# Filling the waits of the first spectral-norm chain and of the first batch's entry with other products, and splitting the first loads of a four-layer convolution and attention kernel

## The chip, the cores and the metric

The kernel runs on one NeuronCore of a Trainium2 chip. The metric is the device time of one execution in microseconds (us). The kernel before takes 1958.89 us (median of three runs, 1958.59 to 1959.13). The profile is one execution of 1957.9 us. Engines are called PE (TensorE, with its weight loads as PEld), DVE (VectorE), ACT (ScalarE), POOL (GpSimd) and SP (SyncE, which here only issues transfers).

## The reference, cut to what matters

Four layers run one after the other on `x` of shape (8, 512, 32, 32) in float32. Only the first two matter for the change:

```python
# layer 0
f = relu(batchnorm(conv1x1(x, Wf)))          # 64 channels, 1024 positions, statistics over the batch
g = relu(batchnorm(conv1x1(x, Wg)))
h = conv1x1(x, Wh)
z = einsum('bcn,bcm->bnm', f, g)             # per batch item
attn = z / svd(z).largest
x = conv1x1(einsum('bnm,bcm->bcn', attn, h), Wv) + x
# layer 1: group norm, then attention over 1024 positions with 512 channels
h = group_norm(x); q, k, v = wq h, wk h, wv h
x = x + wp (softmax(q^T k * scale) applied to v)
# layer 2: a second attention with 128 channels; layer 3: a convolution with signs of x and of its weights
```

## The kernel before, in words

**First pass.** The eight batch items are loaded one after the other (`load_x`, four transfers of 512 KB each, one for each 128 channels, on the SP queue) and multiplied by the three small weights: `fg` for f and g and `h` for h (the loop over `b` with `products`, L1131). For item 0 the loop runs over the four channel chunks outside and over f, g, h inside, so that PE can begin with the first chunk. The weights `fg` (256 KB) and `h` (128 KB) come over the ACT queue, in that order. The results of f and g stay in SBUF, their batch statistics are collected on the way.

**Preparation of layer 1.** Layer 1 uses two folded matrices: `wu`, the product of `wq` and `wk`, and `wo`, the product of `wv` and `wp`. For this `wq`, `wk` and `wv` are first turned (`natural`, eight 128x128 transposes into a two-bank PSUM tile `wide`, then one copy to SBUF), and then multiplied (`product`, L1187: 16 products of 128x128 by 128x512 each; a copy of 128x1024 after each eight, the first on ACT, the second on DVE). `biases` makes two bias vectors with 16 products each that have a single column (L1207, L1222). The main part multiplies in seven block products instead of eight, so it needs sums and differences of the blocks of `wu` and `wo`: `sums_of`, four DVE instructions (L298 to L301).

**The chain.** The largest singular value comes from powers of a 128x128 matrix that holds two batch items: `chain` squares it 2 x 11 times. One step is two products (L935, L936), two copies out of PSUM, one on DVE and one on ACT (L949, L951, or with a scale L953, L957), and then the next step. Every second step is scaled: there a trace goes through a product with a mask (L969), a copy (L970), a reciprocal and two squares on DVE (L996, L997, L999) before the copies may run. There are four such chains; the first one must be finished before the first batch item can enter layer 1. The others run later, spread over the main part. The matrices themselves come from `turned_pair` (transposes of f and g, L1044, copies L1048 on ACT and L1050 on DVE) and `gram` (8 products of 128x128 each, L1241, and a DVE multiplication, L1250).

**The order of PE's work.** From the first chain to the end of the first entry PE's order is written by hand: the code inside `tc.manual_schedule` takes one step of the chain, then two pieces from a generator, `filler`, then the next step. A piece is, for the most part, two products of 128x512 halves or four to eight smaller ones. The other engines' orders are chosen by the framework's scheduler. The pieces come in the order in which `filler` yields them: transposes of `wv`, the product `wu`, the third matrix of the first pair (`gram`), the four sums of `wu` together with `scale_z`, both biases, the matrices of the three other pairs, the product `wo`, the four sums of `wo`.

**The entry.** `entering(0)` then brings the first batch item into layer 1: `weights0` (L274), four times two products and a DVE addition with statistics (`enter`, L393, L402, L405), two small products for the group means (L413, L420), and the square root. Between these steps PE takes the rest of the pieces. After it come the normalization of the item (`normal`, L441 on ACT, L443 on DVE), the differences of its blocks (`split_h`, L309 to L312) and `make_u`, 28 products (L370), with which the main part begins. PSUM holds two `wide` tiles and four single banks in this part.

Of the kernel before, what the change touches and what calls it, by code (L numbers as in the profile page):

```python
# [12 lines left out]
ALU = mybir.AluOpType  # L13
# [70 lines left out]
def kernel(  # L84
# [30 lines left out]
    def wide():  # L115
        return psum["wide"].tile([P, N], F32, tag="wide", name="wide")
# [15 lines left out]
    def load_x(b):  # L132
        t = xpool.tile([P, CC, N], F32, tag="x", name="xt")
        src = x[b].rearrange("(cc p) n -> p cc n", p=P)
        for cc in range(CC):
            nc.sync.dma_start(out=t[:, cc, :], in_=src[:, cc, :])
        return t

    def half(i):
# [16 lines left out]
    early = ctx.enter_context(ExitStack())  # L156
    psum_pools(early, 2, 4)
    a1 = early.enter_context(tc.tile_pool(name="a1", bufs=1))
    load_w("fg", w_fg, [P, CC, P], a1, nc.scalar)
    first = load_x(0)  # L160
    load_w("h", w_h, [P, CC, MID], a1, nc.scalar)


# [934 lines left out]
    def scale_z():  # L1098
# [6 lines left out]
        nc.vector.tensor_tensor(sbw["z"], sbw["z"], ps, ALU.mult)  # L1105


    later = {
        1: [("w3", w_3, a1)],
        2: [("q", w_q, a1)],  # L1110
# [10 lines left out]
    for b in range(B):  # L1121
        xt = load_x(b) if b else first
        for name, src, pool in later.get(b, ()):
            load_w(name, src, shapes.get(name, [P, CC, C]), pool)
        if b >= B - 2:
            resident[b] = xt
        banks = [bank() for _ in w0]

        def products(i, cc):
            for h in range(NH):  # L1130
                mm(  # L1131
                    out=banks[i][side(h), :],
                    lhsT=w0[i][:, cc, :],
                    rhs=xt[:, cc, half(h)],
                    start=cc == 0,
                    stop=cc == CC - 1,
                )

        if b == 0:
            for cc in range(CC):  # L1140
                for i in range(3):
                    products(i, cc)
        for i in range(3):
            if b:
                for cc in range(CC):
                    products(i, cc)
            if i == 0:
                nc.scalar.copy(fs[b], banks[i])
                nc.vector.bn_stats(st[:, 0, b, :], fs[b])
# [12 lines left out]


    nat = {}

    def natural(name, tag):
        t = nat[name] = a1.tile([P, CC, C], F32, tag=tag, name="nat_" + name)
        for i in range(CC // 2):
            tp = wide().rearrange("p (o c j) -> p o c j", o=2, j=P)
            for k in range(2):  # L1170
                for cc in range(CC):
                    nc.tensor.transpose(
                        tp[:, k, cc, :], sbw[name][:, cc, bass.ts(2 * i + k, P)], ident
                    )
            dst = t[:, 2 * i : 2 * i + 2, :].rearrange("p o (c j) -> p o c j", j=P)
            if i % 2:
                nc.vector.tensor_copy(dst, tp)
            else:
                nc.scalar.copy(dst, tp)
            yield  # L1180

    def product(lt, rhs, dst):
        for i in range(CC // 2):
            ps = wide()
            for k in range(2):
                for oc in range(CC):
                    mm(  # L1187
                        out=ps[:, half(k)],
                        lhsT=lt[:, oc, bass.ts(2 * i + k, P)],
                        rhs=rhs[:, oc, :],  # L1190
                        start=oc == 0,
                        stop=oc == CC - 1,
                    )
                    if k == 0 or oc < CC - 1:
                        yield
            to = dst[:, 2 * i : 2 * i + 2, :].rearrange("p o c -> p (o c)")
            if i % 2:
                nc.vector.tensor_copy(to, ps)
            else:
                nc.scalar.copy(to, ps)  # L1200
            yield

    def biases():
        ps = bank()
        for cc in range(CC):
            for oc in range(CC):
                mm(  # L1207
                    out=ps[:, cc : cc + 1],
                    lhsT=nat["k"][:, oc, bass.ts(cc, P)],
                    rhs=col("L1_conv_bq", oc),  # L1210
                    start=oc == 0,
                    stop=oc == CC - 1,
                )
            if cc == 1:
                yield
        nc.vector.tensor_copy(bu, ps[:, 0:CC])
        yield

        ps = bank()
        for oc in range(CC):  # L1220
            for cc in range(CC):
                mm(  # L1222
                    out=ps[:, oc : oc + 1],
                    lhsT=sbw["p"][:, cc, bass.ts(oc, P)],
                    rhs=bvc[:, cc : cc + 1],
                    start=cc == 0,
                    stop=cc == CC - 1,
                )
            if oc == 1:
                yield  # L1230
        nc.vector.tensor_tensor(bo, ps[:, 0:CC], vec("L1_conv_bp"), ALU.add)
        nc.vector.tensor_tensor(bvo, bo, vec("L0_conv_bv"), ALU.add)
        yield

    def gram(j, i, lt, rhs):
        ps = bank()
# [39 lines left out]
    nat_q = natural("q", "w3")  # L1279
    next(nat_q)  # L1280
# [20 lines left out]
    for i in range(2):  # L1301
        for k in range(2):
            relu(2 * jl + k, i)
    next(nat_q)
    nat_k = natural("k", "q")
    next(nat_k)
    next(nat_k)

    def filler():

        yield from natural("v", "k")
        load_w("p", w_p, [P, CC, C], a1, tag="v")
        yield from product(nat["q"], nat["k"], wu)
        yield from gram(jl, 2, ht_pair[jl], gtl)
        cols2 = [slice(0, C // 2), slice(C // 2, C)]
        weights["u"] = sums_of(quarters_of(wu, chunks, cols2), [su[:, i] for i in range(3)])
        scale_z()
        yield
        yield from biases()
        for j in rest:  # L1320
            yield from grams(j)
        yield from product(nat["v"], sbw["p"], wo)
        weights["o"] = sums_of(quarters_of(wo, chunks, cols2), [so[:, i] for i in range(3)])

    todo = filler()
    for _ in range(5):
# [6 lines left out]

    relus = iter([(2 * j + k, i) for j in rest for i in range(2) for k in range(2)])
    with tc.manual_schedule(engines={mybir.EngineType.PE}):
        for _ in chain(jl, True):
            for _ in range(2):
                next(todo, None)
            for args in (next(relus, None),):
                if args:  # L1340
                    relu(*args)
        steps = entering(0)
        for k in range(CC + 2):
            next(steps)
            for _ in range(3 if k < CC else 5):
                next(todo, None)
        for _ in todo:
            pass
# [195 lines left out]
```

## Time and profile before

| | |
|---|---|
| time | 1958.89 us |
| PE busy | 1913.9 us of 1957.9 (98%) |
| DVE, ACT, POOL busy | 1151.2, 512.8, 223.9 us |
| mean granted PE clock | 0.991 |
| first pass, from the first product to the last of h | 5.3 to 96.2 us |
| first chain begins, its last trace product | 113.3 us, 182.2 us |
| first product of `make_u`, end of its last | 211.1 us, 237.3 us |

Busy time of PE includes time at a reduced clock, which the page shows apart ("PEclk"). A stretch in which PE is busy can therefore still be one in which it works at half speed. A matmul row of the profile is one of the passes of a float32 product; two rows make one product of the program.

### The profile page before, as it was taken

To read this page: it belongs to the slowest core of one execution; us is meant where nothing else is said; L and a number is where in the kernel's file an instruction comes from. 1 tells how busy PE (TensorE), PEld (TensorE's weight loads), DVE (VectorE), ACT (ScalarE), POOL (GpSimd) and SP (SyncE) were. 2 spreads that over 40 slices of the span, in tenths; PEclk is the share of its full clock that TensorE was granted. 3 is DMA by queue.
4 is the path that set the end of the run, shared out by engine and by line. 5 is a ranking of instruction groups with operands and counts; after the bars stand their busy time and mean duration, and the time that the engine had idled before them with its cause. 6 is when DMAs were issued, how large, how long until landed. Compare 5 with 4: busy or idle time off the path is not lost.

```text
span 1957.9 us, 16696 instructions
## 1 busy us (share of the span) xinstructions
PE 1913.9 (98%) x6230; PEld 989.2 (51%) x6230; DVE 1151.2 (59%) x1859; ACT 512.8 (26%) x811; POOL 223.9 (11%) x176
## 2 busy tenths in 40 slices
PE   8999899999999999999999999999999999999997
PEld 2377347454565446454455446444645445544653
DVE  3245667537774487637754577447663775466546
ACT  2132122125220342024211332025202421134114
POOL 1000001300021001210112001200120011201110
PEclk9989899999999999999999999999999999999999
DMA  9320000002000020001100120002000110010001
GB/s 337 130 76 1 6 6 12 1 11 86 6 12 1 11 86 17 1 1 46 56 11 0 33 70 12 1 11 86 11 0 1 51 46 11 0 33 22 11 1 56
DMA packets 26712, 66.99 MB, mean 34 GB/s; under 512 B 3760, under 2 KB 4016, under 8 KB 25984
## 3 DMA queue, kind: packets, MB, share of 16 engines
q1 hardware_dynamic: 25968, 65.09, 9.8%
q8 instruction: 51, 0.84, 0.2%
q0 software_dynamic: 224, 0.33, 0.1%
q10 hardware_dynamic: 432, 0.43, 0.1%
q14 instruction: 37, 0.30, 0.0%
HBM read 38.51 MB, written 18.87 MB: 29 GB/s over the span
## 4 chain that ended last, share of the span: by engine, by line
PE 93%; DVE 3%; ACT 2%; DMA 0%; issue 0%; POOL 0%; DVEq 0%; ACTq 0%
PE bank L370 43%; PE bank L537 20%; PE bank L883 6%; PE bank L761 6%; PE bank L1131 4%; PE bank L638 3%; PE bank L655 3%; PE bank L393 2%; PE bank L675 1%; PE bank L935 1%; PE wide L1187 1%; PE bank L1241 1%; PE bank L936 1%; PE bank L782 1%; PE quad L1044 1%; ACT both L699 0%
## 5 line engine op out<-in xcount | busy, mean ns | idle before, releaser
L537 PE MATMUL bank<-e,vt 128*128 128x512 f32 x768 | 334.0, 593 | 0.0
L537 PEld LDWEIGHTS bank<-e,vt 128*128 128x128 f32 x768 | 145.0, 190 | 175.4 <-issue 173.1
L370 PE MATMUL bank<-ut,h 128*128 128x512 f32 x384 | 183.4, 598 | 4.7 <-ACT e L332 4.7
L327 DVE TENSOR_TENSOR e<-bank,e 128x512 f32<-128x512 f32 x128 | 87.6, 684 | 61.5 <-PE bank L370 60.2
L370 PE MATMUL bank<-us,hs 128*128 128x512 f32 x256 | 121.3, 596 | 0.5 <-DVE us L299 0.5
L370 PEld LDWEIGHTS bank<-ut,h 128*128 128x128 f32 x384 | 70.6, 190 | 87.7 <-issue 73.5
L883 PE MATMUL bank<-e,tpg 128*128 128x512 f32 x256 | 114.6, 595 | 0.0
L761 PE MATMUL bank<-tpg 128*128 128x512 f32 x256 | 114.6, 592 | 0.0
L768 ACT ACTIVATE e<-bank 128x512 f32<-128x512 f32 x128 | 76.4, 597 | 128.5 <-PE bank L761 128.5
L370 PE MATMUL bank<-h,wu 128*128 128x512 f32 x192 | 92.1, 603 | 4.9 <-DVE h L443 4.9
L370 PE MATMUL bank<-wo,h 128*128 128x256 f32 x384 | 91.9, 382 | 0.0
L773 DVE TENSOR_TENSOR esum<-esum,e 128x1024 f32<-128x1024 f32 x48 | 58.8, 1225 | 54.9 <-ACT e L768 54.9
L342 POOL TENSOR_TENSOR e<-e 128x512 f32<-128x512 f32 x32 | 41.6, 1301 | 432.2 <-ACT e L321 361.3
L327 DVE TENSOR_TENSOR vt<-bank,vt 128x512 f32<-128x512 f32 x64 | 44.0, 687 | 69.6 <-PE bank L370 69.3
L883 PEld LDWEIGHTS bank<-e,tpg 128*128 128x128 f32 x256 | 48.0, 190 | 63.9 <-issue 63.9
L761 PEld LDWEIGHTS bank<-tpg 128*128 128x128 f32 x256 | 48.6, 190 | 60.7 <-issue 60.5
L370 PEld LDWEIGHTS bank<-wo,h 128*128 128x128 f32 x384 | 71.6, 190 | 14.3 <-ACT vt L321 4.9
L342 POOL TENSOR_TENSOR ut<-ut 128x512 f32<-128x512 f32 x16 | 21.8, 1362 | 477.7 <-ACT ut L323 477.7
L370 PEld LDWEIGHTS bank<-us,hs 128*128 128x128 f32 x256 | 47.3, 190 | 57.5 <-issue 51.4
L790 DVE RECIPROCAL rsum<-bank 128x512 f32<-128x512 f32 x16 | 53.7, 3355 | 30.3 <-PE bank L782 30.3
L665 ACT ACTIVATE sg<-xt,rb 128x512 f16<-128x512 f32 x64 | 43.7, 717 | 103.7 <-DVE xt L657 100.9
L1131 PE MATMUL bank<-xt,fg 128*64 128x512 f32 x256 | 58.6, 608 | 5.3 <-DMA fg<-in_w_fg 5.3
(321 smaller groups left out, 3084.4 us busy)
## 6 DMA issues: line engine op xcount, KB each, us to landing
xt<-in_x SPq DMA_DIRECT2D x56, 512.0 KB
out<-both SPq DMA_DIRECT2D x64, 256.0 KB
rfull<-rsum SPq DMA_DIRECT2D x64, 128.0 KB
f_dram<-f SPq DMA_DIRECT2D x8, 256.0 KB
fb<-f_dram SPq DMA_DIRECT2D x8, 256.0 KB
w<-in_w SPq DMA_DIRECT2D x1, 1024.0 KB
q<-in_w_q SPq DMA_DIRECT2D x1, 1024.0 KB
k<-in_w_k SPq DMA_DIRECT2D x1, 1024.0 KB
```

Source lines behind the costliest of these rows:

```text
L327: nc.vector.tensor_tensor(dst, ps, u, ALU.add)
L342: nc.gpsimd.tensor_tensor(c22, c22, c12, ALU.add)
L370: mm(out=ps[:, q * w : (q + 1) * w], lhsT=lt(ka, kb, q, k), rhs=rhs(ka, kb, q, k), start=first and q == 0 and k == 0, stop=last and k == 1 ...
L537: mm(out=ps, lhsT=a[:, t, bass.ts(r_, P)], rhs=e[t], start=first and t == 0, stop=last and t == NTH - 1, skip_group_check=True,)
L638: mm(out=ps[:, i, :], lhsT=xt[:, cc, bass.ts(4 * h + i, P)], rhs=sbw["tpg"][:, cc, 2 * P : 3 * P], start=cc == 0, stop=cc == CC - 1,)
L655: mm(out=ps, lhsT=sbw["z"][:, bass.ts(oc, P)], rhs=att, start=True, stop=True)
L761: mm(out=ps, lhsT=pt[:, 0, bass.ts(t, P)], rhs=tt[:, 0, half(h)], start=True, stop=True,)
L768: nc.scalar.activation(e[:, half(h)], ps, AF.Exp, scale=float(P) ** -0.5)
L773: nc.vector.tensor_tensor(esum, esum, e, ALU.add)
L790: nc.vector.reciprocal(r, ps)
L883: mm(out=banks[h], lhsT=gt[:, t, :], rhs=es[t][:, half(h)], start=t == 0, stop=t == NT - 1,)
L1131: mm(out=banks[i][side(h), :], lhsT=w0[i][:, cc, :], rhs=xt[:, cc, half(h)], start=cc == 0, stop=cc == CC - 1,)
```

## The change

Nothing of the computation is changed; the same products are made in another order.

- **First loads.** The first 512 KB of `x` come as two transfers of 256 KB (a half of the positions each), and `fg` as four transfers of 64 KB (one per channel chunk), so that the first product can begin when the first pieces have landed. `h` follows `fg` on the same queue as before.
- **`natural`** for `wq` runs inside the first pass, before the last item's products for h; the two halves of each turned tile are copied by ACT and DVE at the same time.
- **The chain's pieces.** After a step without a scale PE takes one piece, after a scaled step two. The sums of `wu` are issued one by one between the pieces of the other pairs' matrices, and so are the biases, now in eight pieces of four products with a PSUM bank and a copy each.
- **`gram`** uses a `wide` tile in place of a single bank.
- **The entry.** Two pieces are taken after each of its first four steps and six after each of the last two, so that the product `wo` comes at the end. Both copies of `wo` are on ACT, and the sums of `wo` are issued after `make_u`.

```diff
-    load_w("fg", w_fg, [P, CC, P], a1, nc.scalar)
-    first = load_x(0)
+    fg = sbw["fg"] = a1.tile([P, CC, P], F32, tag="fg", name="fg")
+    for cc in range(CC):
+        nc.scalar.dma_start(out=fg[:, cc, :], in_=w_fg[:, cc, :])
+    first = load_x(0, True)
     load_w("h", w_h, [P, CC, MID], a1, nc.scalar)
...
         for i in range(3):
+            if b == B - 1 and i == 2:
+                for _ in natural("q", "w3"):
+                    pass
             if b:
...
-            if i % 2:
+            if i % 2 and vector:
                 nc.vector.tensor_copy(to, ps)
...
     def gram(j, i, lt, rhs):
-        ps = bank()
+        ps = wide()
...
-        yield from product(nat["q"], nat["k"], wu)
+        yield from product(nat["q"], nat["k"], wu, True)
         yield from gram(jl, 2, ht_pair[jl], gtl)
-        cols2 = [slice(0, C // 2), slice(C // 2, C)]
-        weights["u"] = sums_of(quarters_of(wu, chunks, cols2), [su[:, i] for i in range(3)])
         scale_z()
         yield
-        yield from biases()
+        between = biases()
+        sums = sums_u()
         for j in rest:
-            yield from grams(j)
-        yield from product(nat["v"], sbw["p"], wo)
-        weights["o"] = sums_of(quarters_of(wo, chunks, cols2), [so[:, i] for i in range(3)])
+            for _ in grams(j):
+                next(sums, None)
+                yield
+                if next(between, "end") != "end":
+                    yield
+        yield from product(nat["v"], sbw["p"], wo, False)
...
-        for _ in chain(jl, True):
-            for _ in range(2):
+        steps = entering(0)
+        for k, _ in enumerate(chain(jl, True)):
+            for _ in range(2 - k % 2 if k <= 2 * NSTEP else 4):
                 next(todo, None)
...
-            for _ in range(3 if k < CC else 5):
+            for _ in range(2 if k < CC else 6):
                 next(todo, None)
...
         ua = got[0]
+        weights["o"] = sums_of(quarters_of(wo, chunks, cols2), [so[:, i] for i in range(3)])
```

More of the change, by code (lines that the diff above doesn't have):

```diff
@@ L130, in psum_pools, with load_x @@
                 )
-    def load_x(b):
+    def load_x(b, split=False):
         t = xpool.tile([P, CC, N], F32, tag="x", name="xt")
@@ L135, in load_x @@
         for cc in range(CC):
-            nc.sync.dma_start(out=t[:, cc, :], in_=src[:, cc, :])
+            for ns in [half(h) for h in range(NH)] if split and not cc else [slice(0, N)]:
+                nc.sync.dma_start(out=t[:, cc, ns], in_=src[:, cc, ns])
         return t
@@ L1105, in scale_z, with natural @@
         nc.vector.tensor_tensor(sbw["z"], sbw["z"], ps, ALU.mult)
+    nat = {}
+    def natural(name, tag):
+        t = nat[name] = a1.tile([P, CC, C], F32, tag=tag, name="nat_" + name)
+        for i in range(CC // 2):
+            tp = wide().rearrange("p (o c j) -> p o c j", o=2, j=P)
+            for k in range(2):
+                for cc in range(CC):
+                    nc.tensor.transpose(
+                        tp[:, k, cc, :], sbw[name][:, cc, bass.ts(2 * i + k, P)], ident
+                    )
+            dst = t[:, 2 * i : 2 * i + 2, :].rearrange("p o (c j) -> p o c j", j=P)
+            nc.scalar.copy(dst[:, 0], tp[:, 0])
+            nc.vector.tensor_copy(dst[:, 1], tp[:, 1])
+            yield
     later = {
@@ L1161, with product @@
             scale_signs(total3)
[L1164 to L1175, printed above, removed]
-            if i % 2:
[L1177 to L1182, printed above, removed]
+    def product(lt, rhs, dst, vector):
         for i in range(CC // 2):
@@ L1196, in product @@
             to = dst[:, 2 * i : 2 * i + 2, :].rearrange("p o c -> p (o c)")
-            if i % 2:
+            if i % 2 and vector:
                 nc.vector.tensor_copy(to, ps)
@@ L1203, in biases @@
     def biases():
-        ps = bank()
[L1205 to L1214, printed above, removed]
-                yield
[L1216 to L1231, printed above, removed]
+        for w, rhs, dst in (
+            (nat["k"], [col("L1_conv_bq", k) for k in range(CC)], bu),
+            (sbw["p"], [bvc[:, k : k + 1] for k in range(CC)], bo),
+        ):
+            for i in range(CC):
+                ps = bank()
+                for k in range(CC):
+                    mm(
+                        out=ps[:, 0:1],
+                        lhsT=w[:, k, bass.ts(i, P)],
+                        rhs=rhs[k],
+                        start=k == 0,
+                        stop=k == CC - 1,
+                    )
+                if dst is bu:
+                    nc.vector.tensor_copy(bu[:, i : i + 1], ps[:, 0:1])
+                else:
+                    nc.vector.tensor_tensor(
+                        bo[:, i : i + 1], ps[:, 0:1], col("L1_conv_bp", i), ALU.add
+                    )
+                yield
         nc.vector.tensor_tensor(bvo, bo, vec("L0_conv_bv"), ALU.add)
-        yield
     def gram(j, i, lt, rhs):
-        ps = bank()
+        ps = wide()
         for t in range(NT):
@@ L1278 @@
         nc.vector.bn_aggr(mv[:, i, :], st[:, i, :, :])
-    nat_q = natural("q", "w3")
-    next(nat_q)
+    nat_k = natural("k", "q")
+    next(nat_k)
     turn(last[0], last[1], ht_pair[last[0] // 2], 0)
@@ L1303, with sums_u @@
             relu(2 * jl + k, i)
-    next(nat_q)
-    nat_k = natural("k", "q")
     next(nat_k)
-    next(nat_k)
+    def sums_u():
+        a11, a12, a21, a22 = quarters_of(wu, chunks, cols2)
+        s1, s2, s4 = (su[:, i] for i in range(3))
+        weights["u"] = {
+            "A11": a11, "A12": a12, "A22": a22, "S1": s1, "S2": s2, "S3": a21, "S4": s4
+        }
+        for args in (
+            (s1, a21, a22, ALU.add),
+            (s2, s1, a11, ALU.subtract),
+            (a21, a11, a21, ALU.subtract),
+            (s4, a12, s2, ALU.subtract),
+        ):
+            nc.vector.tensor_tensor(*args)
+            yield
+    cols2 = [slice(0, C // 2), slice(C // 2, C)]
     def filler():
@@ L1312, in filler @@
         load_w("p", w_p, [P, CC, C], a1, tag="v")
-        yield from product(nat["q"], nat["k"], wu)
+        yield from product(nat["q"], nat["k"], wu, True)
         yield from gram(jl, 2, ht_pair[jl], gtl)
-        cols2 = [slice(0, C // 2), slice(C // 2, C)]
-        weights["u"] = sums_of(quarters_of(wu, chunks, cols2), [su[:, i] for i in range(3)])
         scale_z()
         yield
-        yield from biases()
+        between = biases()
+        sums = sums_u()
         for j in rest:
-            yield from grams(j)
-        yield from product(nat["v"], sbw["p"], wo)
-        weights["o"] = sums_of(quarters_of(wo, chunks, cols2), [so[:, i] for i in range(3)])
+            for _ in grams(j):
+                next(sums, None)
+                yield
+                if next(between, "end") != "end":
+                    yield
+        yield from product(nat["v"], sbw["p"], wo, False)
     todo = filler()
@@ L1341 @@
                     relu(*args)
-        steps = entering(0)
         for k in range(CC + 2):
             next(steps)
-            for _ in range(3 if k < CC else 5):
+            for _ in range(2 if k < CC else 6):
                 next(todo, None)
```

## The prediction

> **What bounds the kernel.** Page first: PE is busy 1913.9 of 1957.9 us and is 93% of the chain that ended last, so the time is PE's work plus PE's waits plus what the clock takes. The instruction order on the engines shows that from the first scores on, PE and DVE of the changed kernel follow the old order, so I look only at the first 240 us. The view of busy time by stretches (us; then busy time and instructions of PE, PEld, DVE, ACT, POOL; granted clock; DMA share; GB/s):
>
> ```profile
> 0.00:5.30 5.30, 0.03 (x2) 0.03 (x2) 0.06 (x1) 1.28 (x1) 4.32 (x14) 1.00 0.65 205
> 5.30:9.00 3.70, 3.65 (x8) 0.74 (x8) 0.00 (x0) 0.00 (x0) 0.45 (x13) 1.00 1.05 289
> 9.00:96.20 87.20, 87.17 (x413) 30.03 (x413) 27.79 (x68) 13.88 (x23) 2.03 (x2) 1.00 0.63 237
> 96.20:113.30 17.10, 14.96 (x113) 12.45 (x111) 8.02 (x23) 12.81 (x18) 0.70 (x1) 1.00 0.45 131
> ...
> 135.30:152.40 17.10, 16.30 (x77) 15.85 (x77) 3.75 (x16) 1.49 (x4) 0.00 (x0) 0.50 0.00 0
> 152.40:182.20 29.80, 29.10 (x245) 27.16 (x243) 16.24 (x64) 6.83 (x18) 0.00 (x0) 1.00 0.01 1
> 182.20:202.40 20.20, 19.01 (x50) 6.89 (x50) 13.98 (x28) 4.03 (x6) 0.00 (x0) 1.00 0.04 14
> 202.40:211.20 8.80, 0.85 (x6) 0.68 (x5) 7.64 (x28) 0.75 (x2) 1.20 (x1) 0.76 0.00 0
> 211.20:217.20 6.00, 5.58 (x7) 1.95 (x8) 5.55 (x7) 2.76 (x5) 0.00 (x0) 0.50 0.00 0
> 217.20:237.30 20.10, 20.10 (x48) 8.98 (x47) 4.64 (x8) 3.33 (x5) 2.52 (x2) 1.00 0.00 0
> ```
>
> Three losses: PE idle to 5.3 us; 17.1 us at half clock in the chain; 8 us without work at 202 to 211, with half clock after it. The list of PE's waits names the releasers:
>
> ```profile
> PE bank L1131 <- DMA fg<-in_w_fg: 5.3, 1, 5.3
> PE bank L370 <- DVE h L443: 4.9, 1, 4.9
> PE bank L420 <- DVE dev L417: 2.5, 1, 2.5
> PE bank L1207 <- DVE z L1105: 1.4, 1, 1.4
> ...
> PE bank L274 <- DVE gm L1014: 0.9, 1, 0.9
> ```
>
> For the first loads, the queue table of the transfer view for 5 to 6 us and for 8 to 9 us (packets, MB, share):
>
> ```profile
> q1 hardware_dynamic: 69, 0.28, 69.4%
> q10 hardware_dynamic: 73, 0.07, 21.0%
> ```
> ```profile
> q1 hardware_dynamic: 62, 0.23, 70.8%
> q0 software_dynamic: 62, 0.07, 25.8%
> q10 hardware_dynamic: 65, 0.02, 9.1%
> ```
>
> q1 carries SP's x in 4 KB packets, q10 what ACT issued in small ones. Both get as many packets in the same time, whatever their size.
>
> **The Trainium skill.** "TensorE: Matmul & The Clock Gate", Part 1, says PE runs at half clock until a window of about 3.4 us was busy, and falls back after an idle one. The trace agrees: full clock from 9.0 us, half clock at 135.3 to 152.4 and 207.0 to 217.2, which are five and three times 3.41 us. "DMA: Bandwidth & Descriptors", "Queues, rings and completion order", says each DMA engine goes round the queues packet by packet; the rows above agree. The TensorE page, in its architectural detail, says ACT and DVE take instructions strictly in order; no row here contradicts it, and I use it for what queues behind a wait.
>
> **Part 1, first loads.** For item 0 PE's order is four products with fg, two with h, then the next chunk. fg's pieces begin it earlier, but h decides when it goes on: before, PE's loads of h weights wait until 9.03 us. h is behind fg on ACT's queue. Per DMA engine fg was 8 packets of 2 KB; now it is 32 of 512 B, each taking turns with a packet of x. So h's 8 packets end beside x's last chunk (16 turns of 2 KB and 24 of 4 KB), not its second. By then x 2.10 MB, fg 0.26, h 0.13 and most of POOL's 0.33 MB have moved, 2.8 MB. The transfer rates of before for each us (0.17 MB by 3 us, then 0.41, 0.39, 0.41, 0.10, 0.36, 0.33, 0.26, 0.29 MB) make 2.7 MB by 11 us, so the estimate is 11.4. Before, the last packet of h ended at 8.1 and PE saw it at 9.03, so add 0.9: 12.3 us. The four products need 3.7 us at half clock as before, begin about 4.2 and end near 8; PE idles over 4 us and restarts at half clock for one window, which costs 3.4/2 = 1.7 us. Sum (12.3 - 9.0) + 1.7 = +5.0 us. Bounds: h at 9.0 as before, with nothing gained, 0; if h drained freely because x's queue ran dry, PE would begin 1 us sooner, -1; one more cold window, +6.5. After it PE never waited for x up to 96 us, and x has more time now.
>
> **Part 2, natural q.** Its 16 transposes (2.1 us) move ahead of h's 3.65 us, and each turned tile now leaves by a 0.56 us ACT copy beside a 0.69 us DVE copy in place of one of 1.01 or 1.23. The waits of the transposes (1.2 and 0.4 us) go, but the statistics (mean, power on POOL, relu on ACT) still end about 8.6 us after h's products against 8.0 us of PE work. Net -0.5 us.
>
> **Part 3, chain to end of make_u.** Before: 113.3 to 237.3 us = 124.0. PE's idle time in it is 12.5 us (in four stretches 0.59 + 0.83 + 0.8 + 0.7, then 1.19 + 7.95 + 0.42) and half clock costs 16.3/2 + 5.6/2 = 10.9 us. Work at full clock: 124.0 - 23.4 = 100.6 us. The products are the same, so this stays, and I count the new waits.
>
> *Pace of the chain.* An unscaled step needs 1.05 us from its first product to the next (118.15 to 119.2), a scaled one 2.05 (154.90 to 156.95). A piece is 0.86 to 0.93 us. PE has 0.44 + 0.9 = 1.3 us in the first and 0.44 + 0.2 + 1.8 = 2.4 in the second, so nothing waits unless DVE is late by more than 0.3 to 0.4 us. The chain and the pieces inside it are 44 us of PE work (23 pairs of 0.44, 12 trace products of 0.2, 34 pieces), not the 69 us from 113.3 to 182.2. The single-column biases, 7 us of work drawn out to 12.4 at half clock, now come 0.9 us at a time between denser products, so I expect full clock.
>
> *What queues on DVE in it.* Three instructions of 0.65 us (two sums of wu and z) stand between trace, reciprocal and squares of one scaled step: 1.3 us of wait. Two bias copies stand ahead of a reciprocal and wait for a piece's end: 0.65 each. A gt copy of 0.69 us ahead of a square: 0.85. The 1.2 us copy of wu, ft copies and the rest: five times 0.25. Together 4.7 us. ACT's relus (0.76 us each) at the start repeat what was there before.
>
> *End of the chain.* From the last trace product to L274 took 3.06 us; 3.6 us of matrices cover it. What remains is 0.5 us for the pv copies, and 0.3: 0.8.
>
> *Entry.* Each of four steps costs DVE 0.75 + 0.69 + 0.73 + 0.69 + 0.21 = 3.07 us; now ft, gt and mask copies, 2.5 us together (2 x 0.69, 4 x 0.29), lie between them. DVE needs about 15.8 us to the last statistics, PE has 4 x 1.06 (L393) + 5.4 (six half matrices) + 2.1 (transposes) = 11.7 of work and holds four banks only, so it waits 4.1.
>
> *Means and root.* The two waits of 2.5 and 4.9 us go: five pieces of wo (4.3 us) stand before L420's product and eleven (9.5 us) after it, against about 5 us for the rest.
>
> *Switch to make_u.* A new wait. Both wo copies are on ACT, the second can start only after the last wo product, and ACT's four h instructions (0.73 each) queue behind it. From that product's end: copy to 1.2 us, chunk 1 at 2.0, its other half at 3.4; DVE, which also has sums of wo in front of L309, makes L309 to 4.7, a sum to 5.4, L310 to 6.6. PE has four products, 3.4 us, so 3.2 are waits. They are short enough to keep the clock.
>
> Sum of new waits 4.7 + 0.8 + 4.1 + 3.2 = 12.8 us against 23.4 of idle and clock before: -10.6 us. Bounds: waits of 8 us (-15) or 17 us (-6).
>
> **Sum.** 1958.9 + 5.0 - 0.5 - 10.6 = 1952.8 us.
>
> **Rivals.**
> *The loads do no harm.* If h lands at 9 us or fg's pieces even gain 1 us, parts 2 and 3 stand alone: 1958.9 - 11.1 - 0.5 = 1947.3 us. For it: only 384 KB on ACT's queue, and DMA at 1 in the first 50 us is a mean. Against: the equal packet counts. Chance 0.30.
> *The clock falls in the chain or the entry, slower than before.* If one-column products count as idle, or the entry's waits fill a window, two spells at half clock as long as the old ones (17.1 and 10.2 us) return their 10.9 us, with loads 5 worse: 1952.8 + 10.9 = 1963.7 us. For it: the clock fell just as biases began. Against: 68% busy windows (182 to 202) kept it, and biases are now a quarter of the work. Chance 0.13.
> *One spell of half clock, or waits at the upper bound*: +4.5 us, 1957.3 us. Chance 0.12.
> The likeliest, 1952.8, has 0.45.
>
> **How the numbers follow.** Around the likeliest the part bounds give 1949 to 1957. A range of 1944.5 to 1959 leaves out the slow rival and little of the fast one's edge. 0.2% is 3.9 us, so faster means below 1955.0: three quarters of the likeliest (0.34), the fast rival (0.30), a sliver of the third: 0.66. Same: the rest of the likeliest (0.11), most of the third and some of the slow one: 0.22. Slower: 0.12.
>
> **What would show it.** The start: PE's wait for h near 12 us, and half clock after it (wrong if the steady run begins at or before 9). First pass 5 us later as a whole. In the chain: 23 steps in 47 to 51 us with clock 1.00, waits for ACT's cur at the steps named. No wait for L443's h, but one for L441's, and for L310's hs. If wo's copies or biases show a spell at 0.50, the second or third rival holds.

## The result, and the profile after

The changed kernel takes 1948.65 us (median of four runs, 1948.13 to 1950.19) against 1958.94 us of the kernel before (1958.59 to 1959.13): 10.3 us less, a ratio of 0.9949 with the 95% interval 0.9932 to 0.9966. The forecast was 1952.8 us in a range of 1944.5 to 1959.0, with faster as the likeliest outcome. Direction and range hold; the gain is larger than the 6.1 us forecast.

Where did it go? With the matmuls of both traces laid side by side from the last one backwards, every one from the first scores product on (238.70 us before, 226.84 us after) comes 11.7 to 11.9 us sooner. So the whole difference arises in the first 240 us. Behind the last matmul 0.7 us is lost again: the last DVE instruction ends 4.7 us before the end of the span before (1953.2 of 1957.9) and 5.4 us after (1941.4 of 1946.8). So the two profiled executions lie 11.1 us apart, and the medians 10.3: the execution of before that was profiled is one of its slower ones (an execution with a span of 1957.9 us on record took 1959.7 us).

The busy time by stretches of the changed kernel (us; then busy time and instructions of PE, PEld, DVE, ACT, POOL; granted clock; DMA share; GB/s), cut at the events that answer those of before:

```profile
4.50:10.10 5.60, 4.30 (x8) 1.43 (x8) 0.00 (x0) 1.28 (x1) 1.24 (x15) 1.00 0.95 244
10.10:99.06 88.96, 88.95 (x429) 31.92 (x430) 29.00 (x70) 15.05 (x25) 2.03 (x2) 1.00 0.61 234
99.06:115.00 15.94, 14.39 (x95) 10.67 (x95) 6.97 (x24) 11.46 (x18) 0.70 (x1) 1.00 0.50 169
115.00:162.70 47.70, 45.76 (x319) 37.77 (x319) 28.47 (x117) 14.92 (x35) 0.55 (x1) 1.00 0.06 22
162.70:168.20 5.50, 4.84 (x37) 3.89 (x37) 2.59 (x10) 2.70 (x5) 0.00 (x0) 1.00 0.01 3
168.20:182.50 14.30, 12.47 (x80) 8.81 (x80) 12.98 (x27) 1.17 (x2) 0.00 (x0) 1.00 0.06 19
182.50:199.50 17.00, 16.99 (x44) 8.35 (x44) 2.29 (x14) 1.01 (x1) 1.02 (x1) 0.90 0.00 0
199.50:204.00 4.50, 2.31 (x6) 0.68 (x5) 4.38 (x9) 4.30 (x6) 0.00 (x0) 1.00 0.00 0
204.00:226.80 22.80, 22.75 (x52) 9.73 (x53) 11.30 (x17) 3.33 (x5) 2.53 (x2) 1.00 0.00 0
```

Read it from the top. The clock records begin at 9.01 us, and the view prints 1.00 for the time ahead of them. PE was at half clock there: eight rows with `fg` took 3.68 us in the kernel before up to 9.0 us and 1.88 us afterwards. PE starts 0.8 us sooner than before, then idles 1.3 us ahead of 10.1 us, and the first pass ends at 99.06 us with the 1.75 us of turned `wq` inside it. The chain (115.0 to 162.7 us) is 47.7 us long at full clock, where the old one took 69 us with 17 us at half clock in it. The entry (168.2 to 182.5 us) waits 1.8 us, there is a short spell of reduced clock behind it (the 0.90), and the 8 us hole at 202 to 211 us of before has become 2.2 us (4.50 - 2.31). The list of PE's waits up to 245 us:

```profile
PE bank L1151 <- DMA fg<-in_w_fg: 4.5, 1, 4.5
PE bank L416 <- DVE mv L415: 1.8, 1, 1.8
PE bank L373 <- ACT ut L335: 1.5, 1, 1.5
PE bank L1151 <- DMA h<-in_w_h: 1.3, 1, 1.3
PE quad L1047 <- DVE z L1108: 0.7, 1, 0.7
PE bank L373 <- DVE h L446: 0.7, 1, 0.7
```

The wait of 2.5 us for the deviations is gone, and that for DVE's h has shrunk from 4.9 to 0.7 us. The wait at the group means (L416, L413 before) has grown from 0.6 to 1.8 us. New are 1.5 us in `make_u` for a copy that stands behind h on ACT, and 1.3 us for the weights h of the first pass. For the last one, the queue table of the transfer view for 7 to 8 us (packets, MB, share):

```profile
q10 hardware_dynamic: 236, 0.14, 50.6%
q1 hardware_dynamic: 41, 0.13, 39.2%
```

q10 is ACT's queue with the small pieces of `fg` and h, q1 is SP's with `x`. Here the small packets did not take turns one for one: nearly six of them went for each packet of `x`. Over 5 to 9 us it was 453 against 182, two and a half for each.

### The profile page after: what moved, and what is told of

The parts are those of the page before. It is cut to its first block, busy times and chain, and to the rows that moved or that the text cites. A ratio compares the mean times of both kernels' runs of the same rounds, so it can differ in the third digit from the quotient of the medians.

```text
span 1946.8 us, 16715 instructions
## 1 busy us (share of the span) xinstructions
PE 1908.0 (98%) x6230; PEld 982.9 (50%) x6230; DVE 1149.2 (59%) x1867; ACT 514.4 (26%) x815; POOL 223.6 (11%) x176
## 4 chain that ended last, share of the span: by engine, by line
PE 93%; DVE 3%; ACT 2%; issue 0%; DMA 0%; ACTq 0%; POOL 0%; DVEq 0%
PE bank L373 43%; PE bank L540 20%; PE bank L886 6%; PE bank L764 6%; PE bank L1151 4%; PE bank L641 3%; PE bank L658 3%; PE bank L396 2%; PE wide L1191 1%; PE bank L678 1%; PE bank L938 1%; PE bank L939 1%; PE bank L785 1%; PE wide L1238 1%; DVE st L408 0%; ACT up L701 0%
```

## The experiments

Medians are device times of several runs beside the kernel before on the same chip (1958.8 to 1959.3 us there). The changed kernel was measured once, beside 1958.94 us of the kernel before, so differences to it compare separate measurements, between which the kernel before itself differs by up to 0.5 us. In the texts quoted, "theory" is the view of the prediction or its correction, "rival" the other one.

### The first loads: four kernels

The first one is the kernel before with only the two splits of the first loads:

```diff
-    load_w("fg", w_fg, [P, CC, P], a1, nc.scalar)
-    first = load_x(0)
+    fg = sbw["fg"] = a1.tile([P, CC, P], F32, tag="fg", name="fg")
+    for cc in range(CC):
+        nc.scalar.dma_start(out=fg[:, cc, :], in_=w_fg[:, cc, :])
+    first = load_x(0, True)
```

> The kernel before with nothing but the split loads of item 0 and of fg. Theory (the weights h land later, since fg's small packets stand ahead of them): first product about 4.5 us, PE's wait for h ends near 10.1 us in place of 9.0, all later work 1.1 us later, 1960.0 us. Rival (an earlier first product is what counts): 0.8 us faster, 1958.1 us. Second rival (what was predicted: h at 12.3 us and a restart at half clock): 5 us slower, 1964 us.

Measured: 1960.02 us (twelve runs, 1957.94 to 1961.31), ratio 1.0002 (0.9994 to 1.0011). No difference can be told. In the trace h comes at 9.99 us, PE waits 1.8 us for it, and the first pass and the chain run 0.95 us late; at the switch the half clock lasts 6.8 us in place of 10.2, which in that execution pays it back.

The second is the changed kernel with the old loads, that is the same diff turned round:

> The changed kernel with the loads of before: fg in one transfer, x in four. Theory: h is awaited until 9.0 us, chain and entry keep what they gained, 1.1 us faster than the changed kernel, 1947.5 us. Rival (the loads are part of the gain): 0.8 us slower than the changed kernel, 1949.4 us.

Measured: 1945.54 us (1945.17 to 1946.33), ratio 0.9931 (0.9914 to 0.9947): 3.1 us faster than the full change. Laid side by side, the first pass comes 0.66 us sooner than in the changed kernel: PE goes on with h at 8.62 us without a wait, but is at half clock until 10.39 us. Another 1.67 us come in one step behind the entry, where the changed kernel's spell of half clock is missing (last section), and 0.65 us behind the last matmul.

The third keeps the splits but sends h right behind the first piece of `fg`:

```diff
     for cc in range(CC):
         nc.scalar.dma_start(out=fg[:, cc, :], in_=w_fg[:, cc, :])
+        if cc == 0:
+            load_w("h", w_h, [P, CC, MID], a1, nc.scalar)
     first = load_x(0, True)
-    load_w("h", w_h, [P, CC, MID], a1, nc.scalar)
```

> The changed kernel, with h loaded right behind the first piece of fg and ahead of the three others. Theory: h lands by 6 to 7 us, before the four products that run at half clock have ended near 8 us, so PE goes on without a wait from 4.5 us; full clock at 9.0 us as before; steady work begins about 0.7 us sooner than before the change and 1.8 us sooner than in the changed kernel, 1946.8 us. Rival (the DMA engines are simply full, so whatever comes first delays the rest): the wait moves to another piece, no gain against the changed kernel, 1948.6 us.

Measured: 1947.32 us (1945.98 to 1948.47). PE's wait for h is gone from its list of waits, and the profiled execution, which has the same spell of half clock as the changed kernel's, runs 1.1 us ahead of it throughout.

The fourth leaves `fg` whole and splits only `x`:

> The changed kernel with fg in one transfer and only x's first chunk in two. Theory: h stands behind 8 packets of fg per engine again, PE's wait for h ends at 8.5 to 9.0 us, 1.1 to 1.6 us faster than the changed kernel, 1947.2 us. Rival (it is x's smaller packets that bring h late, by making more turns): h near 10 us, no difference, 1948.6 us.

Measured: 1946.50 us (1945.48 to 1947.36), with 1947.36 in the profiled execution, again with the spell; it is 1.0 us ahead of the changed kernel throughout.

What follows: the harm of the split loads is h's lateness, about 1 us, and comes from the pieces of `fg` in front of it. It is much less than the 5.0 us forecast, because PE waited 1.3 us and not over 4, and in this execution the clock was not lost. Splitting `x` shows neither harm nor gain.

That the clock was kept is luck. In the six traces with `fg` split and h last, h comes between 9.49 and 10.30 us. The latest one (the kernel of "The second copy of `wo` on DVE" below) waits 2.2 us for it and loses the clock for one window:

```profile
7.47:10.89 3.42, 1.18 (x7) 0.30 (x6) 0.00 (x0) 0.00 (x0) 0.00 (x0) 1.00 1.08 287
10.89:14.30 3.41, 3.41 (x12) 0.98 (x10) 1.23 (x9) 0.00 (x0) 0.92 (x1) 0.50 1.02 380
```

Its first pass ends at 100.95 us, 1.9 us later than the changed kernel's.

### The place of `natural` for `wq`

The changed kernel with the transposes of `wq` and their undivided copies back between the statistics:

```diff
-            if b == B - 1 and i == 2:
-                for _ in natural("q", "w3"):
-                    pass
...
-    nat_k = natural("k", "q")
-    next(nat_k)
+    nat_q = natural("q", "w3")
+    next(nat_q)
```

> The changed kernel with the transposes of wq after the first pass, as before, and the old copies of 1.01 and 1.23 us. The trace of the changed kernel has 0.6 us more between the end of the first pass (less the 1.75 us of transposes) and the chain's start than the kernel before. Theory (the earlier transposes bring nothing, since the statistics set the chain's start, and the finer copies lie among them on DVE): 0.5 us faster than the changed kernel, 1948.1 us. Rival (the prediction's: the waits of the transposes go): 0.5 us slower, 1949.1 us.

Measured: 1948.66 us (1948.06 to 1950.51) against 1948.65: no difference. In its trace the transposes wait 1.2 and 0.4 us for DVE's copies, as before the change, but from 14 us to the middle of the chain the distance to the changed kernel only goes from 1.38 to 1.47 us. The waits came and went without a trace in the sum. The 1.38 us themselves come from the start, where this execution has full clock only from 12.93 us; behind the entry it has no spell of half clock and gets 1.5 us back.

### The pieces in each step of the chain

The changed kernel with two pieces after every step and three or five in the entry, the counts of before:

```diff
-            for _ in range(2 - k % 2 if k <= 2 * NSTEP else 4):
+            for _ in range(2):
...
-            for _ in range(2 if k < CC else 6):
+            for _ in range(3 if k < CC else 5):
```

> The changed kernel with the old counts: two pieces after every step of the chain, three and five in the entry; everything else as changed. Theory (the counts matter because they leave wo for the entry's end): the chain takes about 11 us longer, as it takes in 12 more pieces, the entry loses its waits for banks, but no piece is left behind L423, so PE waits 5 us there and starts make_u at half clock; together 5 to 7 us slower than the changed kernel, 1954.6 us. Rival (the gain is the split of the biases and sums alone): within 1.5 us of the changed kernel, 1948.6 us.

Measured: 1949.94 us (seven runs, 1949.23 to 1954.43), 0.996 (0.9949 to 0.9972): 1.3 us slower than the full change. Four of the seven runs lie at 1949.2 to 1949.9 us, three at 1952.8 to 1954.4. By the median the rival's number fits and the 5 to 7 us of the theory do not. The trace, one of the four, shows what the counts trade. The entry begins 7 us later (173.4 us against 166.4), but all gram pieces are done by then, so DVE has less between its statistics and the wait at the means is 0.6 us. The last product of `wo` ends at 195.1 us, 4.4 us sooner than in the changed kernel. Then PE has run out of work. PE's list of waits:

```profile
PE bank L373 <- ACT h L444: 6.1, 1, 6.1
PE bank L1151 <- DMA fg<-in_w_fg: 4.1, 1, 4.1
PE bank L1151 <- DMA h<-in_w_h: 1.1, 1, 1.1
```

and the stretches around that wait (columns as above):

```profile
196.70:200.11 3.41, 0.00 (x0) 0.00 (x0) 3.41 (x12) 0.00 (x0) 0.00 (x0) 1.00 0.00 0
200.11:206.94 6.83, 5.44 (x6) 2.00 (x7) 6.59 (x11) 3.52 (x5) 0.00 (x0) 0.51 0.00 0
```

Nothing is left for PE while the square root runs, 6 us are idle and 6.8 us follow at half clock; the lead is lost, and 1.7 us more at the first scores product (228.58 against 226.84 us). So the mechanism of the theory is there, the idle PE and the half clock, but it had left out the lead. What the new counts bring is work kept for the one place where PE has nothing else.

### The biases, taken out and put in alone

First the changed kernel with the biases in their two old blocks ahead of the grams (`biases` itself as before):

```diff
-        between = biases()
+        yield from biases()
         sums = sums_u()
...
                 next(sums, None)
                 yield
-                if next(between, "end") != "end":
-                    yield
```

> The changed kernel with the biases as before: two banks, pieces of 8, 8 and 16 single-column products in a row ahead of the other pairs' matrices; counts as changed. Theory (single-column products in a row count as idle to the clock): a spell at 0.50 of 3.4 to 17 us begins with them, 2 to 8 us slower than the changed kernel, 1953 us. Rival (the clock fell before only because of the idle time ahead of the biases): no spell at that place, at most 1 us slower, 1949 us.

Measured: 1953.50 us (ten runs, 1952.09 to 1955.83), 0.9972 (0.9962 to 0.9981): 4.9 us slower than the full change. Its stretches in the chain, and the products there:

```profile
134.52:137.93 3.41, 3.36 (x32) 3.27 (x30) 3.35 (x11) 0.63 (x2) 0.00 (x0) 1.00 0.00 0
137.93:141.34 3.41, 3.41 (x18) 3.41 (x18) 0.16 (x1) 0.00 (x0) 0.00 (x0) 0.50 0.00 0
141.34:155.00 13.66, 12.66 (x61) 12.57 (x60) 4.04 (x17) 1.59 (x4) 0.00 (x0) 0.50 0.01 1
```
```profile
134.96 1.84 PE L1211 MATMUL bank<-ct,nat_k 128*128 128x1 f32 x16
137.41 2.93 PE L1211 MATMUL bank<-ct,nat_k 128*128 128x1 f32 x16
141.48 6.97 PE L1226 MATMUL bank<-bvc,p 128*128 128x1 f32 x32
```

The old 17.1 us at half clock are back. The row 134.52:137.93 matters most: PE's records say 98% busy, and the clock still falls at its end. That is against the rival, since PE was not idle there. Without the single-column products (the bias and two rows of a trace) 39% is left. In this execution the spell behind the entry is missing and h came 0.5 us sooner, so the block costs more in it than the 4.9 us between the medians.

Then the other way round: the kernel before with the new `biases` in small pieces between the gram pieces, and `gram` on the wide banks:

```diff
-        ps = bank()
+        ps = wide()
         for t in range(NT):
...
-        yield from biases()
+        between = biases()
         for j in rest:
-            yield from grams(j)
+            for _ in grams(j):
+                yield
+                if next(between, "end") != "end":
+                    yield
```

> The kernel before with one part of the change: the biases' single-column products in small pieces between the pieces of the gram matrices (which move to the wide banks), everything else as before, the loads too. Theory (the biases in one block make PE's windows count as idle, whatever else the change does): no stretch at half clock between 130 and 160 us, where before had 17.07 us, which took 8.5 us; the chain ends 7 to 9 us sooner; the wait for h near 205 us and the half clock after it stay as before: 1950 to 1953 us. Rival (what ends the half clock in the changed kernel is the other number of pieces in each step of the chain, or the time is bound by the chain's waits for DVE and ACT): a spell stays, or the end of the chain moves by less than 3 us: 1956 to 1960 us.

Measured: 1953.34 us (six runs, 1950.35 to 1957.94), 0.9970 (0.9957 to 0.9982): 6 us faster than before with this part alone. The half clock of 17.1 us has shrunk to one stretch of 3.4 us at 137 us, behind a 1.4 us wait for z, and the last trace product comes at 173.1 us in place of 182.2. So the theory's "no stretch" was met in part: one of five windows is left. The entry begins 9.0 us sooner (176.18 against 185.23 us), `make_u` only 5.2 and the first scores product 6.2 us. The other loss stays: this kernel waits 7.9 us for DVE's h (before, 2.5 for the deviations and 4.9 for h). The spread biases, here together with `gram` on the wide banks, thus bring about half of the whole gain, in both directions of the test.

### The second copy of `wo` on DVE

```diff
-        yield from product(nat["v"], sbw["p"], wo, False)
+        yield from product(nat["v"], sbw["p"], wo, True)
```

> The changed kernel with the second copy of wo on DVE again, as before, so that ACT's part of h no longer queues behind a copy. Theory (the switch waits because h takes the memory of the first pass's weights, which is free only when the last product of wo has read them; the copy's engine matters little): 0 to 1 us slower, 1949.1 us. Rival (the prediction's: ACT's queue is the cause): the waits of 0.7 and 1.5 us at the switch fall to 0.5 together, 1.7 us faster, 1946.9 us.

Measured: 1949.34 us (1947.61 to 1951.39), against 1948.65 no difference beyond the spread. Its profiled execution, 1950.1 us, lost 1.9 us at the start already, as shown above. The switch costs 1.88 us for DVE's h and 0.68 us for ACT's copy, 2.6 us together against 2.2 us; from the start of the last product of `wo` to the first scores product it is 27.7 against 27.9 us, so nothing is won or lost. The gain of 1.7 us that the rival expected is not there. The timeline of ACT and DVE in it says which engine was held by what:

```profile
195.47 2.93 ACT L444 ACTIVATE h<-xt,bi,r_r 128x512 f32<-128x512 f32 x4
201.43 1.23 DVE L1202 COPY wo<-wide 128x1024 f32<-128x1024 f32 x1 [6.90 <-PE wide L1191]
202.63 0.17 DVE L1369 MEMSET ones<- 128x128 f32 x1
```

With the copy gone from its queue ACT writes its part of h at 195.47 us, six microseconds before the last product of `wo` ends. So the memory of h is free, against the theory; it is the order in the queue that holds it. Now DVE's part is the one that stands behind the copy.

### Two pieces ahead of the means

The changed kernel with whole loads, and with two of the pieces moved from behind the first product of the means to ahead of it:

```diff
-            for _ in range(2 if k < CC else 6):
+            for _ in range((2, 2, 2, 4, 6, 6)[k]):
```

> The changed kernel with the first loads whole again, and with two pieces more (the second half of the last gram matrix, one product of wo) ahead of the first product of the means in the first batch's entry. With whole loads and the old place of the pieces: 1945.5 us. Theory (PE waits 1.8 us there because DVE's queue of four steps is behind, and enough products of wo stay behind the second product of the means to cover the square root): the wait goes or falls below 0.3 us, no stretch at half clock begins near 182 to 186 us in any execution, later work 1.5 us sooner, 1943.5 to 1944.5 us. Rival (the pieces only move the wait: the last product of wo ends when it did, and the next matrix copy on DVE stands ahead of the statistics): 1945.5 us, with a wait of over 1 us at the means or at h.

Measured: 1942.98 us (1942.84 to 1943.34), 0.9917 (0.9901 to 0.9934): 16 us faster than before and 5.7 us faster than the change. In PE's timeline neither of the products of the means has an idle time in brackets:

```profile
179.93 1.13 PE L1189 MATMUL wide<-p,nat_v 128*128 128x512 f32 x2
180.98 0.38 PE L414 MATMUL bank<-mv,gmat 128*128 128x4 f32 x2
181.22 5.40 PE L1189 MATMUL wide<-p,nat_v 128*128 128x512 f32 x12
186.45 0.28 PE L421 MATMUL bank<-dev,gmat 128*128 128x4 f32 x2
```

Against the kernel with whole loads only, the shift changes at this place by 1.78 us, the wait of 1.8 us. The theory holds. Another 0.84 us between the two traces come from the start, where the full clock begins at 8.21 us in this one and at 10.39 us in the other. The four runs lie within 0.5 us, closer than those of any other changed kernel; that fits a kernel in which no wait is left that can put the clock down, and the mean clock on record is 0.998 for all four; where the clock was full is known for the profiled one alone (from 8.21 to 1933.3 us).

### The tile of ones filled early

The previous kernel with the tile of ones filled at the start:

```diff
     make_identity(nc, ident)
+    ones2 = const.tile([P, P], F32, tag="ones2", name="ones2")
+    nc.vector.memset(ones2, 1.0)
...
-    ones2 = late.tile([P, P], F32, tag="ones2", name="ones2")
-    nc.vector.memset(ones2, 1.0)
```

> The kernel of the run before this one (whole loads, two pieces ahead of the means: 1942.98 us), with the tile of ones that the main part uses taken from the constants' memory and filled at the very start, instead of from memory that the first pass gives back at the switch. Theory (DVE's part of h has waited since 187 us only because the filling of this tile stands ahead of it in DVE's queue and waits for the last product of wo; h's own memory is free): DVE's h begins before 190 us, PE's 0.7 us wait for it goes; ACT's h still stands behind the copy of wo, so the 1.5 us wait for ACT's ut stays and the second weight chunk waits for ACT: 1942.2 to 1943.0 us. Rival (h's own memory is that of the last product's operands): DVE's h begins after the last product of wo as before, 1943.0 us, and the wait for DVE's h stays at 0.7 us.

Measured: 1942.81 us (1942.61 to 1944.08), the same within the spread. The timeline of DVE, ACT and PE:

```profile
189.36 1.91 DVE L446 TENSOR_SCALAR h<-xt,r_r,bi 128x512 f32<-128x512 f32 x4
194.40 1.01 ACT L1204 COPY wo<-wide 128x1024 f32<-128x1024 f32 x1 [5.86 <-PE wide L1191]
195.31 2.93 ACT L444 ACTIVATE h<-xt,bi,r_r 128x512 f32<-128x512 f32 x4
196.18 1.13 PE L373 MATMUL bank<-h,wu 128*128 128x512 f32 x2 [0.96 <-DVE so L301]
```

DVE's h now begins at 189.36 us, before the last product of `wo` ends, so it was the 0.17 us filling that stood ahead of it: its memory comes free only with that product. The wait then moves to ACT, as expected: PE waits 0.96 us for ACT's first part of h (195.31 + 0.73), which stands behind the copy of `wo`. (The profile names a DVE instruction that had ended; ACT's end fits the time.) What is left of the switch, 0.96 and 1.45 us, waits for ACT. That ACT's order alone holds it was not tested in this kernel.

## Why the prediction was right, and where its sizes were off

**Part 1, loads, +5.0: measured +1.1.** First pass to its end without the moved transposes: 99.06 - 1.75 = 97.31 us against 96.2. This is the term furthest off. The mechanism is right (h behind the pieces of `fg` arrives later, and the kernel with h second and those with whole `fg` take the loss away). The step that failed is "Both get as many packets in the same time, whatever their size": in 7 to 8 us ACT's queue moved 236 packets against 41 of `x`. So h was there at 10.1 us, not 12.3, PE idled 1.3 us and not over 4, and the full clock that began at 9.0 us stayed. (The restart at half clock, 1.7 us of the forecast, did come in one other execution of the same loads, as shown above.) The section of the Trainium skill from which I took the turns, "Queues, rings and completion order" in "DMA: Bandwidth & Descriptors", also says that a turn may drain several descriptors of a queue. Counting one record of the profile as one turn was the prediction's step; the runs do not show what a turn is.

**Part 2, `natural`, -0.5: measured +0.6** (114.96 - 97.31 = 17.65 us against 17.06). Its own reason, that the statistics end after PE's work in any case, makes it zero, and the kernel with the transposes put back says zero.

**Part 3, -10.6: measured -13.5.** Before, chain to end of `make_u` took 124.0 us; its start moved from 113.3 to 115.0 us and its end by 11.8 us, which leaves 110.5. By the terms of the sum, each read as stretch less PE's busy time:

| | forecast, us | measured, us |
|---|---|---|
| waits in the chain | 4.7 | 1.9 (47.70 - 45.76) |
| end of the chain | 0.8 | 0.7 (5.50 - 4.84) |
| entry | 4.1 | 1.8 (14.30 - 12.47) |
| switch to `make_u` | 3.2 | 2.2 (4.50 - 2.31) |
| half clock | 0 | 1.7 (one stretch of 3.4 us) |
| PE's work | 100.6 | 102.2 (what is left) |

DVE's queue in the chain was counted too dear: the waits of a square or reciprocal behind a sum of `wu` or a bias copy mostly did not reach PE. In the entry one wait at L416 was all that reached PE. The spell of half clock was left out of the likeliest case and put into a rival. PE's work was 1.6 us too small, though the same 531 rows stand in both stretches, and where the 1.6 us lie is not shown. The biases are at most a small part of them. In the kernel with blocks 16 of their rows in a row took 1.84 us at full clock and 32 took 6.97 us at half clock, so their pace nearly doubles with the clock, and 64 rows make 7.4 us where the forecast had 7. The ends of matmuls in a profile are modelled, so short waits may be hidden in PE's busy time.

What each part brings is known in part: the biases with `gram` 6.0 us alone, the counts 1.3 us, the loads about -1 us (a loss). By these figures some 4 of the 10.3 us are left (an estimate) for the rest and for what the parts do together. No run took out the sums of `wu` issued one by one, or the sums of `wo` behind `make_u`.

The pace of the chain stands (47 to 51 us at clock 1.00; measured 47.7). Of the signs at the switch, "No wait for L443's h" is wrong: PE waits 0.7 us for it, because a filling that needs old memory was queued ahead of it, which I had not looked for. The wait for L441's h is there as the copy behind it on ACT (1.5 us), and the one for L310's hs never came.

**The rivals.** "The loads do no harm" gave 1947.3 us, nearest to the result, but not for its reason: the loads do harm by about 1 us, and part 3 brought more. The clock's fall in the chain did not happen, though its ground was sound: the 98% row of the kernel with blocks is hard to read otherwise than that single-column products count as idle or nearly so, and spreading them avoids the fall here and, in the kernel before, leaves one window of five. The "68% busy windows" that the prediction set against it (75% in the windows of the clock records) hold products of 512 columns and say nothing of single columns. The third rival's single spell did happen, at a good third of its price (1.7 of 4.5 us).

## What to carry to other kernels

Before adding work to fill waits, mark where PE has nothing else at all (here the square root behind the group means), and save work for that place rather than spending it where the engines nearly keep pace. Spread products that hardly use the array (one column) between dense ones. After a reordering, look at each remaining wait of 1 to 2 us: moving two pieces took away a wait of 1.8 us, and with it the spell of half clock that this wait can cost.

## What the runs showed of the hardware

A wait far shorter than the window can cost a spell of half clock, and by luck. The TensorE page of the Trainium skill, "TensorE: Matmul & The Clock Gate", Part 1, says that the window of 3413 ns runs free of the kernel. The traces agree: all stretches at half clock inside these kernels are 3.41, 6.83, 10.24 or 17.07 us long, and their edges fall elsewhere in each execution. In the changed kernel the 1.8 us wait at the means fell into one window:

```profile
179.68:183.09 3.41, 1.58 (x14) 1.39 (x14) 2.83 (x8) 0.00 (x0) 0.00 (x0) 1.00 0.26 82
183.09:186.50 3.41, 3.41 (x11) 2.22 (x10) 0.82 (x6) 0.00 (x0) 0.00 (x0) 0.50 0.00 0
```

In the kernel with whole loads the same wait lay across the edge of two, and the clock stayed:

```profile
177.65:181.06 3.41, 2.36 (x18) 1.86 (x16) 3.34 (x8) 0.00 (x0) 0.00 (x0) 1.00 0.25 82
181.06:184.47 3.41, 2.62 (x14) 1.91 (x15) 1.64 (x9) 0.00 (x0) 0.00 (x0) 1.00 0.00 0
```

Neither the length of the wait nor PE's busy share as printed decides it. The first of these windows lost the clock with 46% busy. In the kernel with two pieces ahead, this window with a wait of 1.8 us kept it with 47%, while the one of the kernel with blocks lost it with 98%:

```profile
462.18:465.60 3.42, 1.61 (x6) 0.58 (x5) 3.32 (x10) 3.42 (x6) 0.00 (x0) 1.00 0.77 244
```

The two kinds part clearly when the rows with four columns or fewer are left out. In the 13 traces some 7280 windows up to 1930 us, counted from the edges of the clock records, ran at full clock. Thirteen of them were followed by half clock, and in these the other rows kept PE busy for 39% at most; in all the rest they did for 43% at least. So in these traces the line lies between 39% and 43%. It was read from the traces afterwards, and no run was made to test it. It also corrects the prediction, which took both falls of the kernel before for falls after an idle window: in the window ahead of the first (131.97 to 135.38 us) PE was 58% busy, but wider products made only 9%.

A fall of one window costs 3.41 / 2 = 1.7 us (1.67 between the two traces above). This would also explain why one kernel differs by 1.7 us from one execution to the next: the four runs of the kernel with only `x` split are 1945.5, 1945.7, 1947.3 and 1947.4 us. The profiled execution, one of the slower two, shows the spell. The mean clocks on record fit for the others: 0.997 for the slower two and 0.998 for the faster two, and one spell takes 1.7 / 1946 = 0.0009 off the mean. The start has the same luck in it: the first full clock begins between 7.35 and 12.93 us in the 13 traces.
